# A four-layer graph network on one core: a wider rule of urgency and new constants in the kernel's own list planner

## The chip, the cores and the metric

The kernel runs on one core of a Trainium2 chip. The metric is the device time of one execution, in microseconds; lower is better. The core has five engines that each work through their own list of instructions in order: TensorE (PE, matrix products, with its weight loads shown as PEld), VectorE (DVE), ScalarE (ACT), GpSimd (POOL) and SyncE (SP, which here only issues DMA transfers).

## The reference

`x` has shape 64 x 256 x 128 (64 graphs of 256 nodes with 128 features), `adj` is one symmetric 256 x 256 matrix of zeros and ones. Four layers follow each other; each is `x = layernorm(x + layer(x, adj))`, and everything is float32.

```python
# layer 0: h = x @ Wo; e = leaky(u1[idx1] + u2[idx2]); att = softmax(where(adj > 0, e, -9e15), axis=1)
#          att @ h + x @ Wself
# layer 1: h = x @ W; softmax over neighbours of leaky(h@a_src + (h@a_dst)^T); elu(att @ h)
# layer 2: five gated steps, with the same adj for in and out
def step(h, _):
    m_in = jnp.einsum('nm,bmd->bnd', in_matrix, h); m_out = ...   # av = [m_in, m_out]
    u3 = h @ u3_w.T + u3_b
    z = jax.nn.sigmoid(av @ w3_w.T + w3_b + u3)
    r = jax.nn.sigmoid(av @ w4_w.T + w4_b + u3)
    hv = jnp.tanh(av @ w5_w.T + w5_b + (r * h @ u5_w.T + u5_b))
    return (1.0 - z) * h + z * hv, None
# layer 3: y = x W0 + (A x) W1 + (A^2 x) W2 + (A^3 x) W3, both adjacency sets being the same adj
```

## The kernel before

**Units and lanes.** The 64 graphs are cut into 32 units of two graphs. A unit goes through all four layers; ten units are open at a time, one on each of `LANES = 10` sets of buffers. A unit that ends makes room for the unit ten further on.

**Nothing is issued in the order in which it is written.** A function such as `layer2` does not issue instructions; it calls `add(engine, ns, fn, reads, writes, ...)`, which makes a `Task` with its dependencies and an assumed duration. `Plan.run` then plays a list schedule through: at each point of its own clock, each free queue takes, among its tasks that are ready, the one with the smallest key. The result is one fixed order of instructions for each of five queues (`pe`, `act`, `dve`, `pool`, `sp`), and that order is what the chip runs. The constants of the plan (assumed durations, latencies, weights) never reach the chip; they only decide the order.

**The key** is the function `first`. For a unit's task it is the unit's number times `PERIOD` (46000 ns), plus the task's due time within the unit, minus a bonus `soon`. The last ten units stand closer together, `TAIL` times `PERIOD` apart. Due times grow along the dependencies by `PACE` (layer 2: `PACE_GATED`) times the assumed duration and latency of each step.

```python
soon = HASTE.get(t.eng, 0) if t.banks and not t.takes else 0
return (t.unit if t.unit < NU - LANES else NU - 1 - LATE - (NU - 1 - t.unit) * TAIL) * PERIOD + t.due - soon
```

**The bonus and the banks.** PSUM has eight banks. A task that first writes a bank takes a free one (`t.takes`); the bank is free again when its last user has ended. Before the change, the bonus goes to each task on `pe`, `act` or `dve` that touches a bank it did not itself take.

**Latencies.** `Plan.LATENCY` is what the plan adds to a task before its result counts as seen by another queue; after `START` (35 us of the plan's clock) it holds for all, and until then `EARLY` does.

**The lines that the prediction's steps touch.** L533 and L576 are transposes through TensorE, L667, L738 and L743 the products of layer 0, L769, L772 and L773 the attention of layer 1, L780 and L792 its products. In layer 2 each step has products with adjacency blocks (L844, made out of seven 128 x 128 products in `left_fast`; L821 in the early steps of the first two units and the later steps of the last one), then five gate products of 512 columns (`product`, L902), three tanh on ACT (L914, L922, L931), DVE updates (L917, L929, L933, L935), and, for the next step, a transpose of `h` by DVE (L943) and a round trip through DRAM on the SP queue (L946 writes `hb`, four transfers at L949 read `ht`); POOL forms sums of blocks for L844 (L833, L835, L836). Layer 3 multiplies by the weights (L1004), copies half of the result to SBUF on ACT (L1009, L1010), forms the sums on DVE (L833, L835, L836), multiplies with blocks of the squared adjacency (L1015), merges on DVE (L1034, L875, L877, L878, L1038) and normalises: DVE statistics (L587), POOL (L589, L598, L592, L600), four ACT instructions (L611), and the output transfer (L1040). The last `PLAIN` units use `layer3_end` instead, with whole 256-column products (L1051, ACT copies L1055, L1058); of these the last two units normalise with a shorter tail (`layernorm_last`: L629, L630, L632, L634, L636, L639, transfers L642).

Of the kernel before, what the change touches and what calls it, by code (L numbers as in the profile page):

```python
# [30 lines left out]
FIRST_FAR = {0: 2, 1: 2}  # L31
LAST_FAR = {0: 1}
PERIOD = 46000.0
TAIL = 0.3
LATE = 6
PACE = 3.0
PACE_GATED = 1.65
HOLD = 80
DIRECT_ROWS = 3
XDIRECT = 10  # L40
START = 35e3
HASTE = {"pe": 10000.0, "act": 10000.0, "dve": 10000.0}
PLAIN = 3
R2 = 1
R3 = 1.5

# [1 line left out]
class Cell:  # L48


    def __init__(self, ap=None, bank=False, over=()):
        self.ap, self.bank = ap, bank

        self.over = list(over)
        for c in over:
            c.over.append(self)
        self.writers, self.readers, self.users = [], [], 0
        self.group, self.waits = None, set()


class Task:
    def __init__(self, eng, ns, fn, unit, wait, dma):
        self.eng, self.ns, self.fn, self.unit, self.wait, self.dma = eng, ns, fn, unit, wait, dma
        self.step, self.layer = 0, 0
        self.deps, self.then, self.left, self.at = set(), [], 0, 0.0
        self.off = self.end = self.due = 0.0
        self.banks, self.takes = [], []


class Plan:  # L70
# [2 lines left out]

    LATENCY = {"pe": 500, "dve": 400, "act": 400, "pool": 500, "sp": 3500}

    EARLY = {"pe": 250, "dve": 180, "act": 200, "pool": 250, "sp": 2500}
    OWN = {"pe": 0, "dve": 70, "act": 70, "pool": 100}
# [35 lines left out]
    def seen_at(self, t, by):  # L115
        return t.end if t.eng != by.eng or t.dma else t.off + self.OWN[t.eng]

    def run(self, spawn, units, key):

        queue, done_at, order = list(units), {}, []  # L120
        open_units, lane_of = {}, {}
        ready = {e: [] for e in ("pe", "dve", "act", "pool", "sp")}
        free = dict.fromkeys(ready, 0.0)
        seen, now, running = 0, 0.0, []

        def enlist():
            nonlocal seen
            for t in self.tasks[seen:]:
                open_units[t.unit] = open_units.get(t.unit, 0) + 1
                t.left = 0  # L130
                for d in t.deps:
                    if d in done_at:
                        t.at = max(t.at, self.seen_at(d, t))
                    else:
                        t.left += 1
                        d.then.append(t)
                if not t.left:
                    ready[t.eng].append(t)
            seen = len(self.tasks)

        def start(lane):
            mine = [u for u in queue if u % LANES == lane]
            if mine:
                self.unit, self.step = mine[0], 0
                queue.remove(self.unit)
                lane_of[self.unit] = lane
                spawn(self.unit, lane)

                for t in self.tasks[seen:]:
                    t.due = max([d.due + (PACE_GATED if t.layer == 2 else PACE) * (d.ns + (  # L150
                        d.wait + self.LATENCY["sp" if d.dma else d.eng] if d.dma or d.eng != t.eng else self.OWN[t.eng]))
                        for d in t.deps if d.unit == t.unit], default=0.0)
                enlist()

        enlist()
        for lane in range(LANES):
            start(lane)
        while any(ready.values()) or running:

            for t in [t for t in running if t.end <= now]:  # L160
                running.remove(t)
                for c in t.banks:
                    c.users -= 1
                    if not c.users:
                        self.free_banks.append(c.ap)
                open_units[t.unit] -= 1
                if not open_units[t.unit] and t.unit in lane_of:
                    start(lane_of[t.unit])
            for e, tasks in ready.items():
                if free[e] > now:  # L170
                    continue

                fit = [t for t in tasks if t.at <= now + (HOLD if now < START else 0) and len(t.takes) <= len(self.free_banks)]
                if not fit:
                    continue
                t = min(fit, key=key)
                if t.at > now:
                    continue
                tasks.remove(t)
                for c in t.takes:  # L180
                    c.ap = self.free_banks.pop(0)
                order.append(t)
                free[e] = t.off = now + t.ns
                t.end = t.off + (self.EARLY if now < START else self.LATENCY)["sp" if t.dma else e] + t.wait
                done_at[t] = t.end
                running.append(t)
                for n in t.then:
                    n.left -= 1
                    n.at = max(n.at, self.seen_at(t, n))
                    if not n.left:  # L190
                        ready[n.eng].append(n)
            times = [t.end for t in running] + [f for f in free.values() if f > now]
            times += [t.at for tasks in ready.values() for t in tasks if t.at > now]
            times = [x for x in times if x > now]
            if not times:
                assert not any(ready.values()), "the plan is stuck"
                break
            now = min(times)
        assert not queue and len(order) == len(self.tasks)
        return order  # L200
# [3 lines left out]
def kernel(  # L204
# [778 lines left out]
    def layer3(u, L):  # L983
# [11 lines left out]

        if u >= NU - PLAIN:
            layer3_end(u, L, xT, aT, s, tail)
# [44 lines left out]
    def layer3_end(u, L, xT, aT, s, tail):  # L1042
        ps = [bank() for _ in range(NC)]

        def view(c):
            return ps[c].ap.rearrange("p (k b d) -> p k b d", k=2, b=UB)

        for k, src in enumerate((xT, aT)):
            for c in range(NC):
                for b in range(UB):  # L1050
                    add(PE, mm_ns(N), lambda k=k, src=src, c=c, b=b: nc.tensor.matmul(  # L1051
                        view(c)[:, :, b, :], bn(src.ap)[:, b, c * P : (c + 1) * P], w3.ap[:, k],
                        start=(k == 0 and b == 0), stop=(k == 1), skip_group_check=True), (src, w3), (ps[c],), tail)
        for c in range(NC):
            add(ACT, 300, lambda c=c: nc.scalar.copy(s.ap[:, c * N : (c + 1) * N], ps[c].ap[:, 0:N]), (ps[c],), (s,), group=ps)  # L1055
        for c in range(NC):
            for mc in range(NC):
                add(PE, mm_ns(N), lambda c=c, mc=mc: nc.tensor.matmul(  # L1058
                    ps[c].ap[:, N : 2 * N], a2T.ap[:, mc, c * P : (c + 1) * P], s.ap[:, mc * N : (mc + 1) * N],
                    start=False, stop=(mc == NC - 1), skip_group_check=True), (a2T, s), (ps[c],))  # L1060
        pairs = [(ps[c], lambda c=c: view(c)[:, 1]) for c in range(NC)]
        if u >= NU - 2:
            layernorm_last(u, pairs)
            return
        layernorm(u, L, pairs, swap=True)
        add("sp", 450, lambda: nc.sync.dma_start(out_u[u], X[u].ap), (X[u],), ())
# [10 lines left out]
    def first(t):  # L1077
        if t.rank is not None:
            return t.rank * PERIOD
        if t.unit < 0:  # L1080
            return t.due - 1e6
        soon = HASTE.get(t.eng, 0) if t.banks and not t.takes else 0
        return (t.unit if t.unit < NU - LANES else NU - 1 - LATE - (NU - 1 - t.unit) * TAIL) * PERIOD + t.due - soon

    with tc.manual_schedule():
        for t in plan.run(spawn, range(NU), first):
            t.fn()
# [30 lines left out]
```

The softmax here doesn't subtract the row's maximum and nothing guards it: scores larger than these inputs give would overflow.

## Time and profile before

| | |
|---|---|
| time, median of 4 runs | 1389.92 us (1389.27 to 1391.23) |
| time of the profiled execution | 1388.6 us |
| its span, first to last instruction | 1386.6 us |
| granted TensorE clock, mean | 0.999 |
| PE busy, share of the span | 1378.1 us, 99% |
| PEld / DVE / ACT / POOL busy | 70% / 86% / 68% / 45% |
| DMA, mean | 106 GB/s |

Busy times of PE overlap, since one product starts while the one ahead of it is still being finished; what an engine does per unit of time is read from the distance between starts. A float32 product of 128 to 512 columns shows as two records of the matmul engine, a transpose as one. A group's line gives the engine, operation and tiles, the count, the busy time, the mean of one, and the idle time just before with what ended it.

### The profile page before, as it was taken

The numbers are of one execution on the slowest core, as the hardware profiler recorded it, in microseconds if no ns is written. First come the engines' busy times: TensorE is split into PE (matmuls) and PEld (weight loads), VectorE is DVE, ScalarE is ACT, GpSimd is POOL, SyncE is SP. The second block draws the span as 40 slices with busy tenths as digits, with TensorE's granted clock in tenths as the row PEclk, the third lists the DMA queues.
The fourth block names the chain that finished last, engine by engine and source line by source line (L and its number), as shares of the span: only waits on it lengthen the run. The fifth ranks groups of instructions, "written<-read, shape, count | busy, mean of one in ns | idle before, by whom it ended". The sixth has DMA issues, their size and how long they took to land.

```text
span 1386.6 us, 23294 instructions
## 1 busy us (share of the span) xinstructions
PE 1378.1 (99%) x6891; PEld 965.5 (70%) x6891; DVE 1195.2 (86%) x2745; ACT 944.1 (68%) x2303; POOL 626.7 (45%) x1039
## 2 busy tenths in 40 slices
PE   9999999999999999999999999999999999999998
PEld 8776666766666766676766777777666666667777
DVE  7888998998888898888989798899888888998865
ACT  6887656665766677766677678887766655565544
POOL 4134343534355454454354454465444533545433
PEclk9999999999999999999999999999999999999999
DMA  4124544454554554554545555455454454554322
GB/s 134 33 53 98 119 104 105 111 128 111 112 119 107 107 129 100 120 115 105 118 108 115 118 118 117 108 115 117 107 131 98 104 108 94 113 123 114 83 65 61
DMA packets 530077, 147.13 MB, mean 106 GB/s; under 512 B 456480, under 2 KB 495136, under 8 KB 529952
## 3 DMA queue, kind: packets, MB, share of 16 engines
q1 hardware_dynamic: 529152, 145.13, 46.8%
q8 instruction: 55, 0.90, 0.3%
q14 instruction: 70, 0.57, 0.2%
q10 hardware_dynamic: 800, 0.52, 0.1%
HBM read 81.10 MB, written 64.46 MB: 105 GB/s over the span
## 4 chain that ended last, share of the span: by engine, by line
PE 94%; DVE 3%; DMA 1%; POOL 1%; SPq 1%; issue 0%; ACT 0%; POOLq 0%; DVEq 0%; ACTq 0%
PE ps L902 47%; PE ps L844 20%; PE ps L1004 7%; PE ps L743 4%; PE ps L780 4%; PE ps L1015 3%; PE ps L738 2%; PE ps L667 2%; PE ps L792 2%; PE ps L821 1%; PE ps L1051 1%; DMA xT<-hb 0%; DMA ht<-hb 0%; POOL ve L589 0%; PE ps L1058 0%
## 5 line engine op out<-in xcount | busy, mean ns | idle before, releaser
L902 PE MATMUL ps<-m,gT 128*128 128x512 f32 x960 | 478.5, 593 | 0.0
L902 PEld LDWEIGHTS ps<-m,gT 128*128 128x128 f32 x960 | 166.1, 191 | 112.9 <-issue 91.7
L833 POOL TENSOR_TENSOR e<-ht 128x256 f32<-128x256 f32 x121 | 102.5, 847 | 210.3 <-DMA ht<-hb 146.3
L844 PEld LDWEIGHTS ps<-adjTp,ht 128*128 128x128 f32 x726 | 124.0, 191 | 82.7 <-issue 73.1
L914 ACT ACTIVATE e<-ps,bias 128x512 f32<-128x512 f32 x160 | 110.0, 688 | 95.0 <-PE ps L902 89.9
L931 ACT ACTIVATE p<-ps,bias 128x512 f32<-128x512 f32 x160 | 109.9, 687 | 85.9 <-PE ps L902 82.7
L902 PE MATMUL ps<-e,u5T 128*128 128x512 f32 x320 | 163.2, 593 | 0.0
L592 POOL TENSOR_TENSOR rstd<-ve,nhalf 128x4 f32<-128x4 f32 x126 | 142.6, 1133 | 36.7 <-DVE ve L589 31.7
L589 POOL TENSOR_SCALAR ve<-st 128x4 f32<-128x4 f32 x110 | 39.7, 361 | 258.5 <-DVE st L587 229.7
L844 PE MATMUL ps<-adjTp,e 128*128 128x128 f32 x968 | 149.7, 275 | 0.3 <-POOL e L835 0.3
L922 ACT ACTIVATE e<-ps,bias 128x512 f32<-128x512 f32 x160 | 109.9, 688 | 55.7 <-PE ps L902 54.4
L844 PEld LDWEIGHTS ps<-adjTp,e 128*128 128x128 f32 x968 | 130.5, 192 | 14.4 <-issue 11.4
L844 PE MATMUL ps<-adjTp,ht 128*128 128x128 f32 x726 | 138.9, 275 | 0.4 <-DMA ht<-hb 0.3
L933 DVE SCALAR_TENSOR_TENSOR p<-e,p 128x512 f32<-128x512 f32 x160 | 116.0, 726 | 19.8 <-ACT p L931 19.2
L902 PEld LDWEIGHTS ps<-e,u5T 128*128 128x128 f32 x320 | 58.8, 190 | 63.9 <-issue 49.0
L611 ACT ACTIVATE x<-ht,ve,rstd 128x128 f32<-128x128 f32 x212 | 92.3, 489 | 14.6 <-POOL ve L600 14.6
L902 PE MATMUL ps<-xT,gT 128*128 128x512 f32 x192 | 98.0, 593 | 0.0
L875 DVE TENSOR_TENSOR m<-ps,m 128x256 f32<-128x256 f32 x182 | 75.3, 414 | 18.9 <-PE ps L844 17.7
L833 POOL TENSOR_TENSOR e<-x 128x256 f32<-128x256 f32 x61 | 48.5, 795 | 93.9 <-ACT x L611 80.5
L769 ACT ACTIVATE e<-m,esd 128x256 f32<-128x256 f32 x116 | 84.6, 771 | 0.3 <-DMA m<-row 0.2
L917 DVE SCALAR_TENSOR_TENSOR e<-e,xT 128x512 f32<-128x512 f32 x96 | 68.3, 712 | 16.0 <-ACT e L914 15.1
L844 PEld LDWEIGHTS ps<-adjT,x 128*128 128x128 f32 x366 | 60.7, 191 | 29.2 <-issue 24.6
(211 smaller groups left out, 3201.5 us busy)
## 6 DMA issues: line engine op xcount, KB each, us to landing
hb<-p SPq DMA_DIRECT2D x182, 256.0 KB, 2.3
ht<-hb SPq DMA_DIRECT2D x484, 64.0 KB, 2.5
xT<-hb SPq DMA_DIRECT2D x244, 64.0 KB, 2.5
m<-row SPq DMA_DIRECT2D x58, 256.0 KB, 3.7
hb<-p SPq DMA_DIRECT2D x124, 64.0 KB, 1.8
ht<-hb SPq DMA_DIRECT2D x31, 256.0 KB, 2.8
out_dram<-x SPq DMA_DIRECT2D x30, 256.0 KB, 2.5
m<-in_x_dram SPq DMA_DIRECT2D x88, 64.0 KB, 2.4
```

Source lines behind the costliest of these rows:

```text
L592: add(POOL, 1150, lambda: nc.gpsimd.tensor_tensor(rstd.ap, ve.ap, nhalf.ap, op=ALU.pow), (ve, nhalf), (rstd,))
L611: add(ACT, 400, lambda j=j, b=b, ch=ch, view=view, at=at, shift=shift, col=col: nc.scalar.activation(X[u].ap[:, b, ch, :], view()[:, j, :] ...
L769: add(ACT, 660 if u >= DIRECT_ROWS else 360, lambda g=g, b=b: nc.scalar.activation(e.ap[:, g, :].rearrange("p (c n) -> p c n", c=NC), ev() ...
L833: add(by, wide, lambda: eng.tensor_sub(four[:, 0:2], blk(slice(2, 3)).to_broadcast([P, 2, D]), blk(slice(0, 4, 3))), (src,), (s,), group=ss)
L844: add(PE, mm_ns(P) + 4, lambda: nc.tensor.matmul(ps.ap[:, at * P : (at + 1) * P], lhs(), mat.ap[:, k, c * P : (c + 1) * P], start=start, s ...
L875: add(DVE, 335, lambda: nc.vector.tensor_tensor(mv[:, 1:3], pv(y)[:, 0:2], mv[:, 3:4].to_broadcast([P, 2, P]), op=ALU.add), (y, m), (m,))
L902: add(PE, mm_ns(T), lambda: nc.tensor.matmul(ps.ap, w(), rhs.ap, start=start, stop=stop, skip_group_check=True), (c, rhs), (ps,), after)
L914: add(ACT, 590, lambda ps_g=ps_g, up=up: nc.scalar.activation(r.ap, ps_g.ap, AF.Tanh, bias=bias2.ap[:, 1:2], scale=0.5 / up), (ps_g, bias2 ...
L922: add(ACT, 590, lambda ps_g=ps_g, up=up: nc.scalar.activation(z.ap, ps_g.ap, AF.Tanh, bias=bias2.ap[:, 0:1], scale=0.5 / up), (ps_g, bias2 ...
L931: add(ACT, 590, lambda ps_v=ps_v, up=up: nc.scalar.activation(v.ap, ps_v.ap, AF.Tanh, bias=bias2.ap[:, 2:3], scale=1 / up), (ps_v, bias2), ...
L933: add(DVE, 650, lambda: nc.vector.scalar_tensor_tensor(v.ap, z.ap, 1.0, v.ap, op0=ALU.add, op1=ALU.mult), (v, z), (v,))
L1004: add(PE, mm_ns(N), lambda k=k, src=src, c=c, b=b, ps=ps, at=at: nc.tensor.matmul(gd(ps.ap)[:, at], bn(src.ap)[:, b, c * P : (c + 1) * P], ...
```

## The change

The test for the bonus is replaced. A new method `Plan.hold` runs over the tasks of a unit as they are made. For each task it collects, within the unit, the banks that lie at or above it in the graph of dependencies (`after`) and those at or below it (`before`). A task is `within` if some bank stands on both sides and the task does not itself take a bank: so it also marks tasks that touch no bank but lie on a path between two users of one. `first` gives the bonus to these tasks, on all five queues, and the bonus grows from 10000 to 45000 ns. Six other constants get new values. `PLAIN` alone alters what is computed by which instructions: unit 29 goes from `layer3_end` to the ordinary layer 3.

```diff
-TAIL = 0.3
+TAIL = 0.2
-PACE_GATED = 1.65
+PACE_GATED = 1.5
-HASTE = {"pe": 10000.0, "act": 10000.0, "dve": 10000.0}
-PLAIN = 3
+HASTE = {"pe": 45000.0, "act": 45000.0, "dve": 45000.0, "pool": 45000.0, "sp": 45000.0}
+PLAIN = 2
...
-    LATENCY = {"pe": 500, "dve": 400, "act": 400, "pool": 500, "sp": 3500}
+    LATENCY = {"pe": 400, "dve": 350, "act": 350, "pool": 500, "sp": 4000}
...
+    def hold(self, tasks):
+        bits = {}
+        for t in tasks:
+            own = 0
+            for c in t.banks:
+                own |= bits.setdefault(id(c), 1 << len(bits))
+            t.after = t.before = own
+        for t in tasks:
+            for d in t.deps:
+                if d.unit == t.unit:
+                    t.after |= d.after
+        for t in reversed(tasks):
+            for d in t.deps:
+                if d.unit == t.unit:
+                    d.before |= t.before
+        for t in tasks:
+            t.within = bool(t.after & t.before) and not t.takes
...
+                self.hold(self.tasks[seen:])
                 enlist()
...
-        soon = HASTE.get(t.eng, 0) if t.banks and not t.takes else 0
+        soon = HASTE.get(t.eng, 0) if t.within else 0
```

More of the change, by code (lines that the diff above doesn't have):

```diff
@@ L67, in __init__ @@
         self.banks, self.takes = [], []
+        self.after, self.before, self.within = 0, 0, False
 class Plan:
-    LATENCY = {"pe": 500, "dve": 400, "act": 400, "pool": 500, "sp": 3500}
+    LATENCY = {"pe": 400, "dve": 350, "act": 350, "pool": 500, "sp": 4000}
     EARLY = {"pe": 250, "dve": 180, "act": 200, "pool": 250, "sp": 2500}
```

## The prediction

> **What bounds the kernel now.** I read the page's totals, then the chain that ended last, then PE's waits, then the distances between PE's starts, then the last microseconds.
>
> ```profile
> PE 1378.1 (99%) x6891; PEld 965.5 (70%) x6891; DVE 1195.2 (86%) x2745; ACT 944.1 (68%) x2303; POOL 626.7 (45%) x1039
> PE 94%; DVE 3%; DMA 1%; POOL 1%; SPq 1%; issue 0%; ACT 0%; POOLq 0%; DVEq 0%; ACTq 0%
> ```
>
> TensorE is busy without a break and carries 94% of the chain. Busy is not yet "at its rate", so the next lines are pieces of that chain: an uninterrupted row of equal records gives the distance from start to start.
>
> ```profile
> 1014.24 3.46 PE ps L1004 x16
> 1128.41 2.23 PE ps L844 x20
> 1319.79 6.01 PE ps L902 x14
> ```
>
> A record takes 0.216 us at 256 columns, 0.1115 at 128, 0.429 at 512; a product is two records, a transpose one. The program's 3507 TensorE tasks at these rates: 800 products of 512 columns x 0.859, 450 of 256 x 0.432, 1994 of 128 to 130 x 0.223, 128 of 133 x 0.227, 12 of one column x 0.236, 123 transposes x 0.112 = 1371.9 us. The trace has the first product at 1.34 us and the end of the last at 1381.07 (below), 1379.7 us. So of the 1386.6 us span, 1371.9 are products at full rate, 1.3 the wait ahead of them, 5.5 the tail behind them, and 7.8 are all of the delays in the stream. A plan can win from these delays and no more.
>
> ```profile
> PE ps L351 <- POOL ident masks.py:199: 1.3, 1, 1.3
> PE ps L780 <- DVE p L773: 0.5, 1, 0.5
> PE ps L844 <- DMA ht<-hb: 0.3, 1, 0.3
> PE ps L844 <- POOL e L835: 0.3, 1, 0.3
> PE ps L576 <- ACT p L716: 0.2, 1, 0.2
> PE ps L667 <- DVE xT L654: 0.2, 1, 0.2
> ```
>
> Those are all the waits in which PE stood idle. Shorter ones hide under the pipelined ends; the starts show them. Distances over 50 ns longer than the rate add up to 7.9 us in 52 places: 1.7 in the first eight records (3.42 us where 1.73 would do), 1.8 in ten places until 45 us, 2.9 in 22 places ahead of an L844, 0.8 in eight ahead of an L902, 0.4 at an L667, 0.3 in the last three microseconds. The L844 waits look like this one:
>
> ```profile
> 468.21 1.02 PE L902 MATMUL ps<-e,u5T 128*128 128x512 f32 x2
> 469.03 0.45 POOL L835 TENSOR_TENSOR e<-e,ht 128x128 f32<-128x128 f32 x1
> 469.54 0.49 PE L844 MATMUL ps<-adjTp,e 128*128 128x128 f32 x2 [0.30 <-POOL e L835]
> ```
>
> The Trainium skill ("Perfetto Trace Analysis", Identifying the Most-Contended Engine) warns that matmul busy share is a bad measure and that weight-load busy share is a good one; by that, 70% would leave some 30% open. The equal distances above decide otherwise here.
>
> The end, in order of time:
>
> ```profile
> 1378.88 2.19 PE L1058 MATMUL ps<-e,a2T 128*128 128x256 f32 x8
> 1380.74 0.43 DVE L629 BATCH_NORM_STATS2 st<-ps 128x6 f32<-128x256 f32 x1 [2.81 <-PE ps L1058]
> 1383.27 1.04 SPq L642 DMA_DIRECT2D out_dram<-x  x2
> ```
>
> **The change part by part.** The sum is made against the profiled execution's 1388.6 us (span 1386.6 and 2.0 around it), 1.3 below the median of the runs; the difference that I find is added to the median.
>
> *PLAIN.* Unit 29 loses four L1058 (4 x 0.432 = 1.73) and gains seven L1015 (7 x 0.223 = 1.56); its eight L1051 become eight L1004 of the same size. PE: -0.17 us. DVE gets eight more instructions, 2.8 us by their rows (0.28 to 0.42). They are hidden by PE's products of the other units: DVE is busy 51.5 of the 80 us from 1300 to 1380. Without that room they would delay L1015, which is priced below.
>
> *Which tasks are urgent.* Counted over the plan's tasks, the flag goes from 2473 to 2464 on PE, 1312 to 1307 on ACT, 1116 to 1211 on DVE, 0 to 64 on POOL; on SP none has it. So the new test marks nearly the old set. What is new is its weight: 45000 of a 46000 period is one whole unit, where 10000 was a fifth. No instruction is added, no wait either; only the five orders alter, and each queue stays in order, so a task taken early holds up all that stands behind it.
>
> *Latency, pace, tail.* The plan assumed 0.4 to 0.5 us from one engine to the next. The trace has 0.20 from PE to ACT or DVE and 0.03 to 0.09 between the others where the receiver was idle, so 0.35 to 0.40 still covers the hand-over; what is cut is room for queueing. For a transfer the plan's 3.5 becomes 4.0, where the page has 2.3 and 2.5 to landing. A layer 2 step has two transfers in a row, so a next step is planned up to 1 us later. The order of instructions shows both. From a step's last L902 to that unit's next first L844 stand, in PE time at the rates above, over 121 steps: before at least 14.4 us, 2% under 14.7, median 19.0; after at least 15.3, 2% under 15.5, median 19.5. From a unit's last L1004 to its first L1015, where the ACT copies and DVE sums must fit: before at least 1.31, median 2.61; after at least 1.08, median 1.72.
>
> *Worth, L844.* The waits found ahead of L844 are 0.1 to 0.5 us, and the thin steps gain 0.8 to 1.0. I take 2.0 of the 2.9 us away; bounds: nothing, and all 2.9.
>
> *Cost, L1015.* The path from L1004 to the last sum is 0.20 + 0.37 (ACT copy) + 0.41 + 0.28 + 0.28 (DVE) + 0.2 of hand-over = 1.73, and each L1015 has its own shorter part of it. Taking for each unit the L1015 with least PE time to spare over its path: before 0.68 at least, median 1.97; after 0.46 and 0.85. What queueing adds on this path is read in the trace where little was to spare (30 cases under 1.5 us): median 0.15, nine in ten under 0.57, at most 1.03. Most still fit; I take 0.7 us for 30 units. Bounds: 0, and 7.5 if each meets some 0.25 over its reserve. The 0.15 is the nearest row, so I stay near the low end. What PE has queued behind a late L1015 is everything, since its list is in order.
>
> *The start.* Unit 1's first L780, which waited 0.5 on DVE, is reached after 30.4 us of products instead of 33.6, but its own chain is earlier as well: to spare over the bare path 1.05 us against 1.01; unit 0's L780 1.26 against 0.87, its L533 in layer 2 2.8 against 1.3, the L576 that waited 1.48 against 1.02. I take 0.6 of the 1.8 us away; bounds -1.2 and +1.5. Summed over the order by their distances from start to start, DVE has 1.6 and ACT 2.5 us more to do ahead of PE's first 100 us of products than before, with 17 to 22 us to spare.
>
> *The end.* Unit 30 closes the program as before, with four L1051 and four L1058 (8 x 0.431 = 3.45 us) behind unit 29's last L1015. But unit 29 now has the long finish: 0.20 + 1.78 (L1034 to L587, as at 1364.83) + 0.85 (two L587) + 1.78 (POOL) + 0.1 + 1.65 (four L611) = 6.4, that is until 2.9 us after PE's end. Its L611 stand ahead of unit 30's two L636 on ACT, and its power on POOL ahead of unit 30's. Before, the second L636 started 2.4 us after PE's end; now it starts near 3.2. I take +0.8; bounds 0 and +1.5.
>
> Sum: -0.17 - 2.0 + 0.7 - 0.6 + 0.8 = -1.3 us: a profiled execution of 1387.3, a median of 1388.6.
>
> The skill's same page (Optimization Strategy) reads regular bubbles on the saturated engine as a sign that SBUF or PSUM has run out. That speaks against a rule that frees banks sooner: PE's six idle waits name no bank and do not repeat.
>
> **The rivals.** About 0.2%, 2.8 us, is what a measurement of this kernel can tell from no change: under 1387.1 is faster, over 1392.7 slower.
>
> *All waits collected, faster.* L844, L902 and L667 waits gone (-4.1), 1.2 of the start, -0.17, end +0.8, no new wait: -4.7, median 1385.2. For it: the order leaves more between steps nearly everywhere. Against it: L902's distances are as before, and the thin L1015. It takes over if L1015 stays free of waits and 0.9 more of the rest goes.
>
> *L1015 late, slower.* The place is layer 3, 30 times: copies and sums queue on ACT and DVE behind other urgent work of the same rank, and PE stands. Price 7.5 instead of 0.7, so +5.5, median 1395.4. For it: half the reserve is gone. Against it: short delays where the reserve was short before. It decides from 4.8 us in all, 0.16 per unit.
>
> *The rule does not do what it says.* SP has no flagged task and the set is nearly the old one; then the orders differ by small choices only, the waits fall as they fell, and PLAIN and the end are left: +0.6, median 1390.5.
>
> **How the numbers follow.** Forecast 0.48, all collected 0.22, L1015 late 0.22, no effect 0.08. Of the forecast a little reaches over each line: faster 0.25, within 0.2% 0.51, slower 0.24. Range: down to 1385.4, most of the faster case; up to 1394.5, within 1 us of the slower case's 1395.4, whose upper part is left out.
>
> **What would show it.** Right: PE's products again without a break, last product ending 1.5 to 2.5 us sooner, L844 waits under 1 us in all, unit 29's L611 ending shortly before unit 30's L636 starts. Wrong: PE waiting on ACT copies L1009, L1010 or DVE L833 to L836 in many units; a stop of several us anywhere, where TensorE has nothing ready, which the covers above do not show; a tail over 7 us; a granted clock under 0.99.

## The result, and the profile after

The changed kernel takes 1392.12 us (median of 42 runs, 1390.96 to 1393.64), the kernel before 1390.04 (60 runs, 1388.64 to 1392.91): a ratio of 1.0015, 95% interval 1.0011 to 1.0019. It is slower by 2.1 us, where 1.3 us less was forecast. The time lies inside the range and inside the 2.8 us that were called no change, but the runs show a loss. In the changed kernel every line number from L372 on is that of before plus 21 (L844 is L865, L856 L877, L859 L880, L902 L923, L1015 L1036, L611 L632, L636 L657).

The page's totals and the chain that ended last, of the changed kernel:

```profile
PE 1380.5 (99%) x6897; PEld 965.8 (69%) x6897; DVE 1206.5 (87%) x2753; ACT 947.2 (68%) x2304; POOL 635.8 (46%) x1039
PE 95%; ACT 1%; SPq 1%; DVE 1%; DMA 1%; POOL 0%; issue 0%; POOLq 0%; ACTq 0%
```

TensorE bounds the kernel as before. Its waits (line, what it waited for: us in total, times, longest):

```profile
PE ps L372 <- POOL ident masks.py:199: 1.3, 1, 1.3
PE ps L865 <- ACT m L880: 0.6, 1, 0.6
PE ps L1036 <- DVE p L857: 0.5, 1, 0.5
PE ps L554 <- DMA m<-in_x_dram: 0.2, 1, 0.2
PE ps L688 <- ACT ht L691: 0.2, 1, 0.2
```

The prediction's waits on a transfer, on a POOL sum and on layer 1 are gone. Two of those in their place it did not have and matter below: a block product behind an **ACT copy**, and an L1036 (L1015 of before) behind a DVE sum. As before, idle waits are the tip; the sum comes from the distances between TensorE's starts that are over 50 ns longer than the rate (us; in brackets the places, where the two records of one product count as two):

| profiled execution | before | after | difference | predicted |
|---|---|---|---|---|
| products at full rate | 1371.9 | 1371.7 | -0.17 | -0.17 |
| ahead of the block products (L844 of before) | 2.91 (22) | 4.69 (38) | +1.78 | -2.0 |
| ahead of layer 3's second products (L1015) | 0 | 1.03 (6) | +1.03 | +0.7 |
| first 45 us | 3.50 (18) | 3.73 (21) | +0.23 | -0.6 |
| L902, L667, end of the stream | 1.48 (12) | 1.10 (10) | -0.38 | 0 |
| from the last product to the end of the span | 5.57 | 6.67 | +1.10 | +0.8 |
| span | 1386.64 | 1390.23 | +3.59 | -1.3 |

The two spans differ by more than the medians, since the profiled execution of before was one of its quicker ones (in one later set of 33 runs its spans went from 1386.0 to 1388.4, median 1387.2).

**One of the new waits**, the longest, in the timeline of the changed kernel (start, us, engine, line; in brackets idle time and what ended it):

```profile
369.13 0.45 POOL L856 TENSOR_TENSOR e<-e,ht 128x128 f32<-128x128 f32 x1
369.21 0.49 ACT L632 ACTIVATE x<-ht,ve,rstd 128x128 f32<-128x128 f32 x1 [1.51 <-POOL ve L621]
...
369.61 0.24 ACT L880 COPY m<-ps 128x128 f32<-128x128 f32 x1
...
370.00 0.46 PE L865 MATMUL ps<-adjTp,e 128*128 128x128 f32 x2 [0.57 <-ACT m L880]
```

The product at 370.00 multiplies the POOL sum `sm(2)`, which was there at 369.58. It waited for the copy that ended at 369.85, and the copy stood behind an L632 on ACT. That product does not read the copy's result. Of `left_fast`'s seven products it is the third that writes bank `x` (columns 256 to 383); I call it **x2**. The copy (L859 of before) reads columns 0 to 127 of the same bank, and the program makes a product that writes a bank wait for copies out of it issued earlier. The planner has no such dependency, so it may put x2 right behind the copy. In this trace the wait is a separate semaphore instruction, and x2 starts 144 or 145 ns after the copy's end in all 15 places that have it; its second record then starts another 72 or 73 ns late in each of them.

The length of this one wait is not typical. `a_plain3` (below) has the same order here, but the copy starts at 368.68 in its trace and x2 does not wait; the other 14 places are there again, 12 of them within 3 ns of the same length.

The Trainium skill ("PSUM — Partial Sum Buffer", PSUM bank collisions raise a hardware error) says why such an order is kept: two engines must not touch one bank in the same partitions at once, disjoint columns included, and software has to guard by bank, not by address. The traces agree as far as they go (144 ns behind the copy, disjoint columns); a version without the wait was not tried, since it would be a race.

Sorted by which semaphore came last, the 2.91 us ahead of block products before were 1.14 behind a transfer or a POOL sum and 1.77 at nine products behind ACT copies out of bank x (second records counted in). After, they are 0.20 and 4.49 at 18 products. Not all of these are x2: the second product into bank x, **x1**, adds to the columns that the first copy reads, and the plan has that wait as a dependency (`held`). x2 alone went from 1.29 us at seven products to 3.83 at 15, x1 from 0.48 at two to 0.66 at three.

Two runs described below repeat these orders up to their last products and show which of this comes back. `b_plain2`, with the order of before, has x2 at the same seven products (1.66 us), x1 at two (1.10), and no wait at all behind a transfer or a POOL sum. In its list of waits, those ahead of L844 are:

```profile
PE ps L844 <- ACT e L856: 0.7, 1, 0.7
PE ps L844 <- ACT m L859: 0.3, 1, 0.3
```

`a_plain3`, with the order of the changed kernel, has x2 at 14 products (3.14 us), x1 at three (0.91), and 0.44 of the rest. So it is the rise of the x2 waits, from 7 products to 14 or 15, that comes back in the second execution of each order; the 1.14 us does not.

**The end**, in the changed kernel's timeline:

```profile
1384.28 1.65 ACT L632 ACTIVATE x<-ht,ve,rstd 128x128 f32<-128x128 f32 x4 [2.34 <-POOL ve L621]
...
1385.83 0.82 ACT L657 ACTIVATE x<-ps,ve,rstd 128x128 f32<-128x128 f32 x2
1385.95 0.37 SPq L1061 DMA_DIRECT2D out_dram<-x  x1
1386.41 1.01 SPq L663 DMA_DIRECT2D out_dram<-x  x2
```

Unit 29's four normalisations stand ahead of unit 30's two, as predicted, and unit 29's output transfer ahead of unit 30's on SP. Measured from the last product: ACT ends 0.25 us later than before, the last transfer is issued another 0.29 later, and it lands 0.13 later. The ACT delay is less than the 0.8 that the prediction took. The remaining 0.43 come behind the last landing, in the program's closing semaphores (1.314 us against 0.885).

### The profile page after: what moved, and what is told of

Same layout as the page of the kernel before. It is cut to its first block, busy times and chain, and to the rows that moved or that the text cites. A ratio compares the mean times of both kernels' runs of the same rounds, so it can differ in the third digit from the quotient of the medians.

```text
span 1390.2 us, 23348 instructions
## 1 busy us (share of the span) xinstructions
PE 1380.5 (99%) x6897; PEld 965.8 (69%) x6897; DVE 1206.5 (87%) x2753; ACT 947.2 (68%) x2304; POOL 635.8 (46%) x1039
## 4 chain that ended last, share of the span: by engine, by line
PE 95%; ACT 1%; SPq 1%; DVE 1%; DMA 1%; POOL 0%; issue 0%; POOLq 0%; ACTq 0%
PE ps L923 48%; PE ps L865 20%; PE ps L1025 7%; PE ps L764 4%; PE ps L801 4%; PE ps L1036 3%; PE ps L759 2%; PE ps L813 2%; PE ps L688 2%; PE ps L842 1%; DMA m<-in_x_dram 1%; PE ps L1072 0%; ACT x L632 0%; ACT e L790 0%; PE ps L989 0%
## 5 line engine op out<-in xcount | busy, mean ns | idle before, releaser
L923 PE MATMUL ps<-m,gT 128*128 128x512 f32 x960 | 475.2, 593 | 0.0
L923 PEld LDWEIGHTS ps<-m,gT 128*128 128x128 f32 x960 | 167.8, 191 | 127.5 <-issue 106.4
L865 PEld LDWEIGHTS ps<-adjTp,ht 128*128 128x128 f32 x726 | 123.1, 191 | 75.6 <-issue 66.6
L923 PE MATMUL ps<-e,u5T 128*128 128x512 f32 x320 | 163.5, 592 | 0.0
L865 PE MATMUL ps<-adjTp,e 128*128 128x128 f32 x968 | 150.5, 276 | 0.6 <-ACT m L880 0.6
L865 PEld LDWEIGHTS ps<-adjTp,e 128*128 128x128 f32 x968 | 130.5, 192 | 14.7 <-issue 11.2
L865 PE MATMUL ps<-adjTp,ht 128*128 128x128 f32 x726 | 138.0, 275 | 0.1
L632 ACT ACTIVATE x<-ht,ve,rstd 128x128 f32<-128x128 f32 x216 | 94.1, 487 | 18.1 <-POOL ve L621 17.8
L923 PEld LDWEIGHTS ps<-e,u5T 128*128 128x128 f32 x320 | 58.6, 190 | 62.2 <-issue 49.7
L923 PE MATMUL ps<-xT,gT 128*128 128x512 f32 x192 | 98.2, 593 | 0.0
L854 POOL TENSOR_TENSOR e<-x 128x256 f32<-128x256 f32 x61 | 52.3, 858 | 93.4 <-ACT x L632 87.0
L896 DVE TENSOR_TENSOR m<-ps,m 128x256 f32<-128x256 f32 x182 | 74.7, 412 | 12.5 <-PE ps L865 11.6
L856 POOL TENSOR_TENSOR e<-e,ht 128x128 f32<-128x128 f32 x121 | 81.3, 672 | 6.7
```

What stands on the lines that cost most here:

```text
L632: add(ACT, 400, lambda j=j, b=b, ch=ch, view=view, at=at, shift=shift, col=col: nc.scalar.activation(X[u].ap[:, b, ch, :], view()[:, j, :] ...
L854: add(by, wide, lambda: eng.tensor_sub(four[:, 0:2], blk(slice(2, 3)).to_broadcast([P, 2, D]), blk(slice(0, 4, 3))), (src,), (s,), group=ss)
L856: add(by, narrow, lambda: eng.tensor_sub(four[:, 2:3], four[:, 1:2], blk(slice(0, 1))), (src, s), (s,), group=ss)
L865: add(PE, mm_ns(P) + 4, lambda: nc.tensor.matmul(ps.ap[:, at * P : (at + 1) * P], lhs(), mat.ap[:, k, c * P : (c + 1) * P], start=start, s ...
L923: add(PE, mm_ns(T), lambda: nc.tensor.matmul(ps.ap, w(), rhs.ap, start=start, stop=stop, skip_group_check=True), (c, rhs), (ps,), after)
```

## The experiments

Theory: what the change lost is mostly x2 waiting behind ACT copies, because the new constants put it there, with the tail and a later L1015 as the rest. Rival: no single mechanism; any new order of the five queues lands on some other set of short stalls, and the kernel before is one of the better draws. Each run was timed beside the kernel before, and all ratios below are to those runs of it; its median moved between 1389.1 and 1390.0 from set to set, so runs are compared by ratio, not by median. An edit that makes the planner play its schedule anew is a **replanning**; one that touches the finished order alone is **in place**.

### 1. The end, and the missing dependency put into the plan

`a_plain3` is the changed kernel with one constant set back; its order is the changed kernel's up to the last 2% of the products.

```diff
-PLAIN = 2
+PLAIN = 3
```

> The kernel after, with PLAIN back at 3; all but the last 61 tasks of the order stay as they are. Theory (two losses: unit 29's long finish ahead of unit 30's at the end, and in the stream an ACT copy that the plan does not count ahead of an L844 product): the tail behind the last product goes from 6.6 us back to about 5.5, PE work grows by 0.17, so the median falls by 0.9 us to about 1391.2; the distances ahead of L844 over 50 ns stay at 4.7 us in all. Rival (the longer tail comes from the new order of the last units, not from unit 29's layer 3): tail stays over 6.4 us, median 1392.1 or 1392.3.

Measured: 1391.54, ratio 1.0013 (1.0005 to 1.0022), tail 6.00, distances 11.2 us with 4.49 ahead of block products. By ratios the end is worth 0.3 us, which is not clear of the noise; by the tail it is 0.67 less 0.17 of products. It is not the bulk. It is also a repetition: the same order gave 10.5 and 11.2 us of distances, with 4.69 and 4.49 ahead of block products, and 0.80 and 1.63 at L902. Below some 0.8 us a single line of this ledger says nothing.

`a_dep` (changed kernel), `a_dep_plain3` (with PLAIN 3 too) and `b_dep` (kernel before) give the plan the dependency that the chip's program has:

```diff
-        add(ACT, 160, lambda: nc.scalar.copy(gd(m.ap)[:, 0], x.ap[:, 0:P]), (x,), (m,), group=ms)
+        read = [add(ACT, 160, lambda: nc.scalar.copy(gd(m.ap)[:, 0], x.ap[:, 0:P]), (x,), (m,), group=ms)]
...
-        one(x, 2, sm(2), 2, 1, (s,))
+        one(x, 2, sm(2), 2, 1, (s,), read)
```

> The kernel after, with one more dependency in the plan: in left_fast the third product into bank x (of the sum four[:, 2]) comes after the ACT copy out of bank x. The program waits there already; only the plan did not know. Theory: the waits behind the copies L856 and L859 ahead of this product (2.75 us in 15 places over 50 ns) go, distances over 50 ns ahead of L844 fall from 4.7 us to under 2.5, median falls by 2.2 us to about 1389.9. Rival A (the loss is queueing that the shorter latencies no longer cover, at L1004 to L1015 and everywhere): the waits move to other lines, total of distances over 50 ns stays at 10 to 11 us, median within 0.6 us of 1392.1. Rival B (the product was placed well and the extra dependency costs room): slower by 1 us or more.

> Both of the edits in one: the added dependency and PLAIN at 3. Theory: the two gains add up, 1392.1 - 2.2 - 0.9 = 1389.0 us, which is below the kernel before (1390.0). Rival A: only the end is won, 1391.2. Rival B: 1392 or more.

> The kernel before, with the same added dependency. Theory: 0.7 us of waits in six places behind these copies go, median falls by 0.5 us to about 1389.5, less than in the kernel after since there the product follows the copy closely more often (57 of 182 against 33). Rival A: within 0.5 us of 1390.0 either way. Rival B: slower by 1 us or more.

Measured: `a_dep` 1400.18, ratio 1.0071 (1.0058 to 1.0083); `a_dep_plain3` 1400.56, 1.0073 (1.0061 to 1.0086); `b_dep` 1388.41, 0.9991 (0.9982 to 1.0000). TensorE's longest waits in `a_dep`:

```profile
PE ps L923 <- DVE m L899: 3.2, 3, 1.6
PE ps L923 <- ACT e L935: 2.7, 4, 1.4
...
PE ps L865 <- POOL e L856: 1.1, 1, 1.1
```

The dependency did its work: x2 waited at one product in `a_dep` (0.29 us), two in `a_dep_plain3` (1.34) and one in `b_dep` (0.46). But in the changed kernel the new order made gate products wait for DVE's merge and ACT's tanh, 9.1 us in 25 places, and x1 waited 2.15 us at five products. The expectation for `a_dep` missed by 10 us: a replanning is no clean test of one wait. `b_dep` is the fastest order of all runs; of the waits ahead of L844 one of 0.2 us is left in its list (the wait at L351 is left out):

```profile
PE ps L780 <- DVE p L773: 0.5, 1, 0.5
PE ps L667 <- DVE xT L654: 0.4, 1, 0.4
PE ps L902 <- DVE m L878: 0.3, 1, 0.3
PE ps L576 <- DVE cu L674: 0.3, 1, 0.3
PE ps L844 <- ACT m L859: 0.2, 1, 0.2
```

### 2. The wait taken away in place

`a_push` keeps the changed kernel's finished order. It only moves an x2 later on TensorE's list until 1500 ns of other products lie between it and the product whose result the second copy reads, or until something needs it.

```diff
+ROOM = 1500
...
+    def later(order):
...
+            if id(t) in hold and cover[id(hold[id(t)][1])] < ROOM:
+                parked.append(t)
+                continue
...
-        for t in plan.run(spawn, range(NU), first):
+        for t in later(plan.run(spawn, range(NU), first)):
```

> The kernel after with its order kept, but for 28 products: in left_fast the third product into bank x is moved down TensorE's list, at the latest to ahead of its first dependent, until 1500 ns of products stand between it and the product whose result the ACT copy reads. The orders on ACT, DVE, POOL and SP are the same, as is the plan. Theory (this product waits for a copy that the plan does not count): products with under 900 ns in between fall from 27 to 11, the 2.75 us of waits behind copies L856 and L859 fall to under 1, the median by about 1.8 us to 1390.3. Rival A (queueing everywhere; the wait is only found by the next product): the waits move to the products behind, total of distances over 50 ns stays over 10 us, median 1392.

Measured: 1391.22, ratio 1.0007 (0.9998 to 1.0016); span 1388.2 instead of 1390.2. The waits of x2 behind the second copy went from 2.74 us at ten products to none, those behind the first copy stayed (1.75 and 1.94, x1 counted in), the tail stayed at 6.67 and L902 rose from 0.80 to 1.64; all distances together fell from 10.5 to 8.4. One place, first in the changed kernel, where x2 started at 130.75 though the L801 ahead of it took TensorE only until 130.57 at its rate, then in `a_push` (line numbers two to four higher), where other products follow it at once:

```profile
129.92 0.38 PE L865 MATMUL ps<-adjTp,ht 128*128 128x128 f32 x2
130.14 0.60 PE L801 MATMUL ps<-p,x 128*128 128x256 f32 x2
130.34 0.27 ACT L880 COPY m<-ps 128x128 f32<-128x128 f32 x1
130.75 0.46 PE L865 MATMUL ps<-adjTp,e 128*128 128x128 f32 x2
```

```profile
129.64 0.60 PE L803 MATMUL ps<-p,x 128*128 128x256 f32 x2
129.84 0.27 ACT L883 COPY m<-ps 128x128 f32<-128x128 f32 x1
130.07 0.38 PE L867 MATMUL ps<-adjTp,ht 128*128 128x128 f32 x2
130.29 1.06 PE L867 MATMUL ps<-adjTp,e 128*128 128x128 f32 x8
```

This is the clean test of the mechanism: this one class of waits vanished. By ratios it is worth 0.0008 of 1390, 1.1 us where 1.8 were expected, about half of the loss. The two intervals overlap, so the size is not shown; the span of 1388.2 does not show it either, since this profiled execution was 1.2 us quicker than the run's median.

`b_push` is the same in the kernel before; `a_push2` holds x2 back from both copies (the `hold` list takes two pairs for each x2), and `a_push2_plain3` sets PLAIN to 3 as well.

> The kernel before with the same holding back on TensorE behind the second copy only (15 products have less than 900 ns of cover there, against 27 in the changed kernel). Theory: the 0.9 us that these products and their followers wait go, the waits ahead of block products fall from 2.9 to 2.0 us, the median to 1389.1. Rival (holding back costs as much as it saves): 1389.9.

> The changed kernel's order, in which the bank-x product (the third into its bank) is held back on TensorE until 1500 ns of other products lie between it and the product whose result either ACT copy (L877 or L880) reads; the run before held it back from the second copy only. Nothing else moves. Theory (the product waits for the copy of its own bank): its waits behind the first copy, 0.8 us in five places, go as those behind the second went; the waits ahead of the block products fall from 2.1 to about 1.3 us, the median to 1390.4. Rival (any disturbance of TensorE's list gives back elsewhere what it takes away): no lower than the run before, 1391.2.

> The same with PLAIN = 3, so that unit 29 ends as before the change. Theory (bank-x waits and the longer tail together are most of what the change lost): tail 6.0 us instead of 6.7, median 1389.9, within 0.3 of the kernel before. Rival (the end is no cause; what is left sits in the start and in layer 3): as the other run, 1390.4.

Measured: `b_push` 1388.51, 0.9996 (0.9987 to 1.0005), distances ahead of block products 1.24; `a_push2` 1390.32, 1.0009 (1.0000 to 1.0018), 2.03; `a_push2_plain3` 1390.60, 1.0011 (1.0002 to 1.0020), 1.99, tail 6.00. The first is near its expectation, though its interval includes no change. In the second the five x2 waits behind the first copy became one of 0.17 us, but x1 then waited longer for that copy (0.39 us at 662, 0.20 at 912), so nothing was gained over `a_push`: there the rival was right. In the third the tail was 0.68 us shorter and the time no better. In-place repair reaches 1.0007 and no further; in these traces the rest is spread over L902, L1015, x1 and the end.

### 3. One part of the change at a time

`b_plain2`, `b_tail2`, `b_lat_eng`, `b_lat_sp` and `b_lat` are the kernel before with one edit each; `b_rule45` takes the new test (`hold`, `within`) with the bonus of 45000 on five queues, and none of the other constants. `a_tail3` and `a_lat` are the changed kernel with one edit undone. Besides the bonus the change gives seven numbers new values: `TAIL`, `PACE_GATED`, `PLAIN` and four latencies. `PACE_GATED` was neither set alone nor taken back, and the new test was not run without the larger bonus, so what each of these does is open.

```diff
b_plain2:   -PLAIN = 3
            +PLAIN = 2
b_tail2:    -TAIL = 0.3
            +TAIL = 0.2
b_lat:      -    LATENCY = {"pe": 500, "dve": 400, "act": 400, "pool": 500, "sp": 3500}
            +    LATENCY = {"pe": 400, "dve": 350, "act": 350, "pool": 500, "sp": 4000}
b_lat_eng:  +    LATENCY = {"pe": 400, "dve": 350, "act": 350, "pool": 500, "sp": 3500}
b_lat_sp:   +    LATENCY = {"pe": 500, "dve": 400, "act": 400, "pool": 500, "sp": 4000}
a_tail3:    -TAIL = 0.2
            +TAIL = 0.3
a_lat:      -    LATENCY = {"pe": 400, "dve": 350, "act": 350, "pool": 500, "sp": 4000}
            +    LATENCY = {"pe": 500, "dve": 400, "act": 400, "pool": 500, "sp": 3500}
```

> The kernel before with the new rule and its bonus of 45000 on all five queues, every other constant old. Theory: 14 products with under 900 ns (15 before), so no loss of this kind: within 0.7 us of 1390.0. Rival C (the bonus of a whole unit makes the losses): 1391.5 or more.

> The kernel before with the new LATENCY alone. Theory: 27 products with under 900 ns as in the kernel after (15 before), waits behind the copies up by about 2 us, none of the longer tail: 1391.5 to 1392. Rival C: 1390, no change.

> The kernel after with the old LATENCY (0.5, 0.4, 0.4, 3.5 us). Theory: it is the cut of the latencies that brings the product close behind the copy; under 900 ns stand 11 of 182 such products instead of 27, waits ahead of L844 of this kind fall under 1 us, the median falls by 1.5 to 2 us to about 1390.4, with the longer tail kept. Rival C (the bonus of one whole unit makes the losses): 1392 as before.

> The kernel before with PLAIN = 2 and nothing else; TensorE's order is the same up to its last tasks. Theory (the end costs 0.8 us less 0.17 of products): tail 6.3 to 6.7 us instead of 5.6, median 1390.4 where the kernel before has 1389.8; the waits ahead of block products stay near 2.9 us. Rival (the end is hidden): 1389.6.

> The changed kernel with TAIL = 0.3. Theory (unit 29's long finish meets unit 30's only because TAIL = 0.2 brings the units together): tail 5.5 to 5.7 us instead of 6.7; the first 752 us have the same order and so the same waits; median about 1391, 1 us under the changed kernel. Rival (PLAIN alone makes the tail, the short one in the kernel before was luck): tail 6.3 or more.

> The kernel before with TAIL = 0.2 and nothing else. Theory: with PLAIN = 3 the tail is 6.0 us, as in the changed kernel with PLAIN = 3; products of the bank-x kind with under 900 ns of cover 17 (15 before), so the waits ahead of block products within 1 us of 2.9; median 1390 to 1391 where the kernel before has 1389.6. Rival (TAIL has no part in the tail): 5.6 us.

> The kernel before with the engines' new latencies (PE 400, DVE and ACT 350 ns), the transfer's left at 3500. By the count (9 products with under 900 ns of cover, 15 before): waits behind the copies 1.0 to 1.8 us, not more than before. If shorter assumed hand-overs leave TensorE waiting for ACT and DVE in general, L902 waits rise to 3 us or more and the median to 1393; if not, it is 1389.5.

> The kernel before with the transfer's new latency alone (4000 instead of 3500 ns). By the count (12 products, 15 before): waits behind the copies 1.0 to 2.0 us. If the transfer's latency is the part that costs, L902 waits of about 5 us and a median near 1396; if it is the engines' part, 1389.5.

Measured, with the kernels of the case for comparison ("short x2" is the number of x2 behind the second or first copy with under 900 ns of products in between, counted in the order before a run; of 182):

| run | median | ratio (95%) | distances, all | behind ACT copies (products) | of it x2 (products) | short x2 | tail |
|---|---|---|---|---|---|---|---|
| before | 1390.04 | 1 | 7.9 | 1.8 (9) | 1.3 (7) | 15 | 5.57 |
| after | 1392.12 | 1.0015 (1.0011-1.0019) | 10.5 | 4.5 (18) | 3.8 (15) | 27 | 6.67 |
| b_plain2 | 1389.65 | 1.0004 (0.9995-1.0014) | 9.1 | 2.8 (9) | 1.7 (7) | 15 | 5.64 |
| b_rule45 | 1389.54 | 0.9998 (0.9989-1.0007) | 8.9 | 3.0 (7) | 1.3 (4) | 14 | 5.87 |
| b_tail2 | 1392.18 | 1.0020 (1.0011-1.0030) | 11.8 | 2.7 (9) | 1.4 (6) | 17 | 5.89 |
| b_lat_eng | 1392.04 | 1.0018 (1.0010-1.0027) | 11.0 | 1.0 (4) | 0.8 (3) | 9 | 6.01 |
| b_lat_sp | 1392.48 | 1.0021 (1.0012-1.0029) | 11.6 | 4.3 (11) | 3.1 (6) | 12 | 5.51 |
| b_lat | 1398.27 | 1.0061 (1.0047-1.0074) | 16.7 | 4.1 (18) | 3.3 (14) | 27 | 6.27 |
| a_tail3 | 1393.83 | 1.0030 (1.0018-1.0043) | 12.4 | 4.2 (13) | 2.4 (9) | 22 | 6.25 |
| a_lat | 1406.49 | 1.0119 (1.0105-1.0133) | 22.1 | 7.2 (16) | 3.2 (8) | 11 | 9.80 |

*The rule alone*, with its bonus, is worth nothing that these runs can measure. Its expectation held; a loss appeared only where other constants changed as well.

*The latencies* do not add up. The engines' part alone costs 0.0018 x 1390 = 2.5 us, the transfer's part 2.9, both together 8.5, and taking both back in the changed kernel costs 14 more, where 2 us less was expected. `b_lat` was expected at 1391.5 to 1392 and missed by 6 us: its x2 waits rose as expected, but 5.1 us stood ahead of L902 as well. `b_lat_eng` and `b_lat_sp` fit neither of the times set for them (1389.5 or 1393, and 1389.5 or 1396), and `b_tail2` and `a_tail3` were 1 to 3 us slower than expected. The longest waits of TensorE in `a_lat`:

```profile
PE ps L865 <- ACT e L877: 2.8, 5, 1.1
PE ps L923 <- ACT e L935: 2.2, 5, 1.0
PE ps L865 <- DVE m L886: 1.4, 1, 1.4
```

These are waits behind ACT and DVE instructions; the first line is x1 behind the first copy, which the plan has as a dependency. The single edits differ in kind too. `b_lat_eng` lost at the end and in layer 1, `b_lat_sp` behind copies:

```profile
PE ps L1058 <- ACT e L1055: 1.6, 2, 1.3
```

```profile
PE ps L844 <- ACT m L859: 1.2, 2, 1.0
```

*The count of short x2* was right for `b_lat_eng` (9, expected 1.0 to 1.8 us behind copies, measured 1.0) and wrong for `b_lat_sp` (12, expected 1.0 to 2.0, measured 4.3) and for `a_lat` (11, expected under 1, measured 7.2, of it 4.0 at x1). In the two runs with 27 the x2 waits are the longest, 3.8 and 3.3 us; in `b_lat_sp` and `a_lat` they are nearly as long at half as many products. The count finds x2 that stand too near; it does not see how late a copy runs.

*The tail* is not PLAIN's, nor TAIL's. `b_plain2` has the same long finish of unit 29 and a tail of 5.64:

```profile
1382.16 1.65 ACT L611 ACTIVATE x<-ht,ve,rstd 128x128 f32<-128x128 f32 x4 [0.98 <-POOL ve L600]
...
1383.76 0.46 ACT L636 ACTIVATE x<-ps,ve,rstd 128x128 f32<-128x128 f32 x1
```

There the four instructions are through when unit 30's first is due. In that order 4.75 us of unit 30's products stand behind unit 29's last L1015, three L1051 more than the changed kernel's 3.45. `a_tail3` has 3.45 again and its tail is 6.25: the expectation of 5.5 to 5.7 missed, its rival's 6.3 was nearer. So in these three profiles the term is there where unit 29 ends 3.45 us of products before the program does, and 1.3 us more takes it away. The 0.43 us behind the last landing are a matter of their own. The closing semaphores took 1.31 to 1.33 us in the changed kernel, `a_plain3`, `a_dep`, `a_dep_plain3`, the three `a_push` and `b_lat_eng`, 1.37 in `a_lat`, 1.18 in `b_lat` and `b_rule45`, and 0.88 in the kernel before and the other six. That looks like a property of the program, but each has one profile, and what sets it stays open.

**What follows.** Ten replannings with another constant, rule or dependency were run: the changed kernel, `a_dep`, `a_lat`, `a_tail3`, `b_dep`, `b_rule45`, `b_tail2`, `b_lat`, `b_lat_eng` and `b_lat_sp`. Eight are slower, by 1.5 to 12 thousandths, one is equal, and one is 1.2 us faster with an interval that ends at no change. Their stalls sit in different places each time. For the changed kernel the place is known and was tested in place; why its constants lead there, and not to `a_lat`'s 14 us or `b_rule45`'s nothing, is not one cause that these runs could isolate. No version beats the kernel before beyond doubt; `b_dep`, `b_push` and `b_rule45` beat the changed kernel.

## Why the prediction was wrong

- **"Worth, L844" is the step that failed**: -2.0 us forecast, +1.8 measured. It read the 2.9 us as waits like the one it showed, on a POOL sum, and booked on them the 0.8 to 1.0 us more room that the new order leaves between a step's last L902 and the next step's first L844. But only 1.14 of the 2.91 stood behind transfers and POOL sums. They became 0.20; whether the room did that is not shown, since `b_plain2` has none of them with the order of before. The other 1.77 stood behind ACT copies out of bank x, among the block products themselves, where that room does not count. Of it 1.29 was x2, whose wait is not among the plan's dependencies. The x2 with under 900 ns of room rose from 15 to 27, and the x2 waits from 1.29 us to 3.83 (in the repeats, 1.66 and 3.14). The prediction's "no wait either" overlooked that x2 waits for a copy only where the order issues it behind that copy: behind the second one 33 of 182 times before, 57 after. The lower bound of the term, "nothing", was wrong too: a replanning can add waits of the class that it is meant to remove.
- **"Cost, L1015"** was right in kind and near in size: +0.7 forecast, +1.03 in six places, one of them 0.64 behind a DVE sum. In four more runs of almost that order it was 0.93 to 1.44; before's order had none in one profile and 0.57 in the other (`b_plain2`). The rival that priced it at 7.5 did not come.
- **"The start"**: -0.6 forecast, +0.2 measured with the first eight records. Between them and 45 us, four profiles with before's order in this stretch had 1.81, 1.96, 2.38 and 2.38 us of distances, and six with the changed kernel's 1.56, 1.69, 1.83, 2.10, 2.13 and 2.45. The means, 2.14 and 1.96, differ by 0.2 in the forecast direction, inside the scatter: a term of 0.6 us was more than one profile could carry.
- **"The end"**: +0.8 forecast, +1.10 measured, and the nearness is luck. The forecast was 0.8 of delay on ACT, and 0.25 came; 0.42 came through SP and the landing and 0.43 through the closing semaphores, which the prediction did not name. Unit 29's long finish accounts for 0.67 (`a_plain3`, without it, has a tail of 6.00).
- **PLAIN's products**, -0.17: right. The DVE instructions that it adds cost nothing visible.
- **"The rule does not do what it says"** was closest, at 1390.5 and with a chance of 0.08. `b_rule45` shows that it described the rule well; of the constants it priced only `PLAIN`.
- **The base**: the difference was taken from one profile of before with 7.9 us of distances. Another execution with that order up to its last products (`b_plain2`) has 9.1, so terms under half a microsecond were beyond what one profile resolves.

## What to carry to other kernels

Sort the stalls of the bounding engine by the semaphore that ended each, not by the line they stand ahead of, before a gain is booked on them; and count the covers over the waits that the program has, bank hazards included, not over the planner's own dependencies. When a list schedule is played anew, expect a new set of stalls: where TensorE already stands at 99%, eight of ten new orders here were slower. A wait is tested cleanly by moving the one instruction in the finished order. And take two profiles of one order before a stall is priced: the waits that the gain was booked on were missing from the second.

## What the runs showed of the hardware that was not expected

A product that waits for a copy in its bank started 143 to 146 ns after the copy's end where the wait was a separate semaphore instruction, and 52 to 54 ns after where it was not; its second record then started another 72 or 73 ns late in the first case and 101 or 102 in the second. The program's closing semaphores took from 0.88 to 1.37 us after the last landing; in the changed kernel one drain in them lasts 221 ns, where the kernel before has one of 78, but `a_lat` took the 1.37 with a drain of 78.
